# A graph layer with quantile aggregation: neighbour lists and gathered rows in place of sorted tables

## The chip, the core and the metric

The kernel runs on one core of one Trainium2 chip. The core has five engines with instruction streams of their own: PE (TensorE, matrix products into PSUM), DVE (VectorE), ACT (ScalarE), POOL (GpSimd) and SP (SyncE, which here only issues DMAs), and 16 DMA engines. The metric is the device time of one execution in microseconds, as the median of several runs; lower is better.

## What is computed

For 16 graphs (batches) of 1024 nodes with 64 channels: layer norm and relu; then for each node the weighted sum of the 0.25, 0.5 and 0.75 quantiles, per channel, of its kept neighbours' values, itself included; the node's own value is added, a two-layer MLP and a residual follow.

```python
h = jnp.maximum(_layernorm(x, axis=-1), 0.0)
# inside the layer, with x = h:
neigh = (adj_ > 0) & ~eye
rank = jnp.cumsum(ni, axis=-1) - ni
nb = ni.sum(-1)
skip = jnp.where(nb > T, (nb + K - 1) // K, 1)              # T = 10, K = 2
rem = neigh & (sk > 1) & (rank % sk == sk - 1) & mask[:, :, None]
rem = rem | jnp.swapaxes(rem, 1, 2)
adj_d = jnp.where(rem, 0.0, adj_)
vals = jnp.where(nd[..., None], x[:, None, :, :], jnp.inf)
s = jnp.sort(vals, axis=2)
nv = nd.sum(2)
for tau, w in zip((0.25, 0.5, 0.75), (0.25, 0.5, 0.25)):
    pos = tau * (nv - 1)                                      # lo, hi = floor, ceil; frac = pos - lo
    agg = agg + w * (v_lo + frac * (v_hi - v_lo))
y = jax.nn.relu((x + agg) @ W1 + b1) @ W2 + b2
# and at the end
x = x + y * mask
```

The adjacency is a symmetric random one, drawn with probability 1/256 for each direction; a node has 8 neighbours on average.

## The kernel before

It finds the order statistics for any adjacency, with no list of neighbours. For a pair of batches, `prep_pair` does the layer norm (L129 to L143), transposes to channels on 128 partitions, and sorts all 1024 values of each channel with a bitonic network on DVE (L181 to L191, with the node numbers as payload), then sorts back (L216, L217) to give each node's rank. For a batch, `prep_batch` loads the adjacency in 8 tiles of 128 rows (L244), makes it 0 or 0.5 on DVE (L246), clears the diagonal on POOL (L247, `affine_select`), counts neighbours with a scan (L254), marks the dropped edges (L266, L267, L270), puts the diagonal back (L271, POOL) and transposes on PE (L301, L302).

`main` computes a batch in 192 units: 16 groups of four channels, two halves of the nodes and six order statistics. PE multiplies the kept adjacency with weights built from the ranks (`pack`, L374); for each unit `choose`, `words`, `locate` and `add` pick the bucket, select its counts and words (`sel`, L397), move bits (L404), compare (`hit`, L418), weight the hit on POOL (`hitw`, L420), multiply with the candidates (`val`, L422) and sum into `agg` on PE (L426). The units are written as a software pipeline of four stages; one step of the next batch's preparation (`background`) is taken per unit.

The source is written against a layer that places the waits between engines, hands out the buffers (a tile's `bufs` is how many copies of it can be alive) and orders the instructions of each engine when the kernel is built; an engine then works through its own list in that order. DMAs are issued by SP alone. On POOL are the products `wt` (L365) and `hitw`, the coefficients (L339, L340) and the two diagonal masks.

Of the kernel before, what the change touches and what calls it, by code (L numbers as in the profile page):

```python
# [29 lines left out]
I32 = mybir.dt.int32  # L30
U8 = mybir.dt.uint8
AF = mybir.ActivationFunctionType
OP = mybir.AluOpType
AX = mybir.AxisListType

P = 128
N = 1024
C = 64
H = 128
NT = N // P  # L40
NG = 16
NB = 32
HALF = 512
NSEL = 6
WEIGHTS = (0.25, 0.5, 0.25)
EPS = 1e-5
FIELDS = ((0, 11), (11, 11), (22, 10))


@with_exitstack  # L50
def quantile_graph_layer(
# [24 lines left out]
    kb = cst.tile([P, cbf.shape[1]], BF16, name="kb")  # L76
    nc.sync.dma_start(out=kb, in_=cbf)
    kf = cst.tile([P, cf32.shape[1]], F32, name="kf")
    nc.sync.dma_start(out=kf, in_=cf32)
# [30 lines left out]
    # Sorted tables of four groups each, block-diagonal over a group's four channels.  # L110
# [6 lines left out]
    xs, hT, rankT, sorted_d = {}, {}, {}, {}  # L117
    nd, bucket, word_w, maskc = {}, {}, {}, {}

# [1 line left out]
    def prep_pair(pr):  # L121
        xt = wk.tile([P, NT, 2, C], F32, name="xt")
        xs[pr] = xt
        for b in range(2):
            nc.sync.dma_start(out=xt[:, :, b, :], in_=x[2 * pr + b].rearrange("(t p) c -> p t c", p=P))
# [69 lines left out]
        # The sorted values as three bf16 terms.  # L195
# [13 lines left out]
        # Node numbers back in order, each with the place it was found at.  # L209
# [24 lines left out]
    def prep_batch(b):  # L234
        mu = wk.tile([P, NT], U8, name="mu")
        nc.sync.dma_start(out=mu, in_=nodemask[b].rearrange("(t p) -> p t", p=P))
# [5 lines left out]
        for t in range(NT):  # L242
            at = wk.tile([P, N], F32, name="at")
            nc.sync.dma_start(out=at, in_=adj[b, t * P:(t + 1) * P, :])  # L244
# [7 lines left out]
            # Half the inclusive count of neighbours; the dropped ones are those numbered skip, 2 skip.  # L252
# [16 lines left out]
            # 0.5 for a kept edge, 1 for a dropped one, 0 for none.  # L269
# [37 lines left out]
    def main(b, background):  # L307
# [12 lines left out]
        # The order statistics that each node wants, and their weights, on all partitions.  # L320
# [47 lines left out]
        def pack(wt, half):  # L368
            """Counts below (less a half) and the three words, for all buckets of four channels."""
# [25 lines left out]
        def words(packed, hot):  # L395
# [6 lines left out]
            # 2^23 + word: each partition moves its bit to where it reads as 2.0.  # L402
# [69 lines left out]
        nc.sync.dma_start(out=out[b].rearrange("(t p) c -> p t c", p=P), in_=res)  # L472

    def drain(gen):
        for _ in gen:
            pass

    drain(prep_pair(0))
    drain(prep_batch(0))
    for pr in range(B // 2):  # L480
        batch = prep_batch(2 * pr + 1)
        pair = prep_pair(pr + 1) if pr + 1 < B // 2 else iter(())
        main(2 * pr, chain(batch, pair))
        drain(batch)
        # The next pair's first batch takes over what the batch before left free.
        batch = prep_batch(2 * pr + 2) if pr + 1 < B // 2 else iter(())
        main(2 * pr + 1, chain(pair, batch))
        drain(chain(pair, batch))


def constants():
    """Matrices that depend on the shapes alone."""
# [21 lines left out]
    ci32 = np.stack([30 - inside, np.ones(P)], 1).astype(np.int32)  # L514
    return cbf, cf32, ci32
# [25 lines left out]
```

## Time and profile before

| | us |
|---|---|
| median of three runs | 18756.4 |
| lowest and highest run | 18733.7, 18758.3 |
| profiled execution, span from first to last instruction | 18769.8 |

The profile is of one execution. Its first lines give each engine's busy time; its groups give, for a line of the kernel and an engine, the count of instructions, their busy time, the mean duration, and the idle time of the engine ahead of them with what ended it. "128x512 f32" is partitions x elements per partition. A view of a single line gives the shortest, median and longest duration. In a timeline a row is start, duration, engine, line and operation, with the engine's idle time ahead of it in brackets.

### The profile page before, as it was taken

How to read it: one execution, taken by the hardware profiler on the slowest of the kernel's cores; microseconds unless marked ns; L12 is line 12 of the kernel's file. 1: busy time of each engine (PE TensorE's matmuls, PEld its weight loads, DVE VectorE, ACT ScalarE, POOL GpSimd, SP SyncE). 2: the span in 40 equal slices, each digit the busy share in tenths (PEclk: the TensorE clock that was granted, in tenths of full speed). 3: DMA queues.
4: the chain of work that ended last, by engine and by line, in shares of the span. 5: the costliest groups of instructions: out<-in, count | busy, mean ns of one | idle time of the engine just before them, and what ended most of it. 6: DMA issues, size and time to landing. Idle time of an engine off the chain costs nothing. (4 is left out here: it accounts for less than half of the span.)

```text
span 18769.8 us, 153006 instructions
## 1 busy us (share of the span) xinstructions
PE 15007.5 (80%) x55296; PEld 5255.5 (28%) x55296; DVE 15816.9 (84%) x19847; ACT 3137.9 (17%) x5402; POOL 7256.0 (39%) x4293
## 2 busy tenths in 40 slices
PE   2887788777888788887788887888878887788888
PEld 0222222222222222222222222222222222223333
DVE  9898878988789887898878988789887898877777
ACT  0111111111111111111111111111111111111111
POOL 1333443334433344333443334433343333443333
PEclk6999999999999999999999999999999999999999
DMA  0000000000000000000000000000000000000000
GB/s 23 4 1 3 10 8 4 1 3 12 8 2 1 3 12 8 2 1 3 12 8 2 1 3 12 8 2 1 3 12 9 1 2 2 12 6 1 2 1 1
DMA packets 183963, 98.46 MB, mean 5 GB/s; under 512 B 163426, under 2 KB 163618, under 8 KB 183202
## 3 DMA queue, kind: packets, MB, share of 16 engines
q1 hardware_dynamic: 183202, 88.68, 1.8%
q8 instruction: 433, 7.09, 0.2%
q14 instruction: 328, 2.69, 0.0%
HBM read 78.14 MB, written 10.49 MB: 5 GB/s over the span
## 5 line engine op out<-in xcount | busy, mean ns | idle before, releaser
L420 POOL TENSOR_TENSOR hitw<-hit,coef 128x512 bf16<-128x512 bf16 x3072 | 5080.3, 1654 | 9836.9 <-DVE hit L418 9596.5
L426 PE MATMUL agg<-val,kf 128*64 128x512 f32 x6144 | 3445.6, 643 | 2079.5 <-DVE val L422 2071.6
L374 PE MATMUL pk<-kept,wt 128*128 128x512 fp8e4 x16384 | 4170.5, 385 | 278.2 <-POOL wt L365 155.5
L397 DVE TENSOR_TENSOR sel<-packed,hot 128x2048 f16<-128x2048 f16 x3072 | 4090.9, 1335 | 123.3 <-ACT hot L392 115.6
L422 DVE TENSOR_TENSOR val<-cand,hitw 128x512 f32<-128x512 f32 x3072 | 2113.5, 688 | 1976.9 <-POOL hitw L420 1884.2
L401 PE MATMUL wd<-sel,kb 128*128 128x512 f16 x9216 | 2650.1, 391 | 744.4 <-DVE sel L397 742.6
L392 ACT CAST hot<-oh 128x512 f16<-128x512 f32 x3072 | 1797.1, 585 | 7573.1 <-PE oh L390 3841.7
L416 PE MATMUL cand<-hot,table 128*128 128x512 f16 x9216 | 2674.7, 396 | 0.0
L404 DVE TENSOR_SCALAR bits<-wd,ki 128x512 int32<-128x512 int32 x3072 | 2278.7, 742 | 124.4 <-PE wd L401 122.2
L378 ACT ACTIVATE packed<-pk 128x512 f16<-128x512 f32 x2048 | 1223.2, 597 | 6859.8 <-PE pk L374 6858.1
L418 DVE TENSOR_TENSOR hit<-place,want 128x512 bf16<-128x512 f32 x3072 | 2099.5, 683 | 319.2 <-PE place L413 308.0
L374 PEld LDWEIGHTS <-wt 128*128 128x128 fp8e5 x16384 | 1593.4, 99 | 2507.5 <-POOL wt L365 380.5
L365 POOL TENSOR_TENSOR wt<-eq,ww 128x1024 fp8e5<-128x1024 bf16 x768 | 1824.9, 2400 | 724.0 <-DVE eq L362 473.2
L426 PEld LDWEIGHTS agg<-val,kf 128*64 128x64 f32 x6144 | 599.5, 137 | 3576.8 <-DVE val L422 3447.8
L401 PEld LDWEIGHTS <-kb 128*128 128x128 bf16 x9216 | 921.1, 100 | 2088.2 <-issue 1155.6
L413 PE MATMUL place<-bits,kb 128*128 128x512 bf16 x3072 | 1253.2, 408 | 97.9 <-DVE bits L404 96.8
L390 PE MATMUL oh<-below,kb 128*128 128x512 f16 x3072 | 1197.6, 390 | 163.8 <-ACT hot L392 137.9
L383 DVE TENSOR_TENSOR below<-packed,want 128x1536 f16<-128x1536 f16 x1024 | 1254.7, 1225 | 3.9 <-ACT want L337 3.4
L416 PEld LDWEIGHTS <-table 128*128 128x128 bf16 x9216 | 869.5, 100 | 1325.0 <-issue 629.9
L411 PE MATMUL place<-sel,kb 128*128 128x512 f16 x3072 | 1215.8, 396 | 14.6 <-DVE hit L418 14.4
L399 PE MATMUL wd<-hot,kb 128*128 128x512 f16 x3072 | 1200.9, 391 | 0.0
L413 PEld LDWEIGHTS <-kb 128*128 128x128 bf16 x3072 | 304.1, 99 | 1512.5 <-issue 1402.5
(97 smaller groups left out, 7443.2 us busy)
## 6 DMA issues: line engine op xcount, KB each, us to landing
at<-in_adj_dram SPq DMA_DIRECT2D x128, 512.0 KB, 3.6
table<-sd SPq DMA_DIRECT2D x768, 8.0 KB, 1.7
sd<-term SPq DMA_DIRECT2D x24, 256.0 KB, 2.0
xt<-in_x_dram SPq DMA_DIRECT2D x16, 256.0 KB, 4.0
out_dram<-res SPq DMA_DIRECT2D x16, 256.0 KB, 2.6
kb<-in_cbf_dram SPq DMA_DIRECT2D x1, 320.0 KB, 2.7
mu<-in_nodemask_dram SPq DMA_DIRECT2D x16, 1.0 KB, 4.7
kf<-in_cf_dram SPq DMA_DIRECT2D x1, 126.0 KB, 2.6
```

The source lines that it names most:

```text
L365: nc.gpsimd.tensor_tensor(dst(n + 1), eq, wb, OP.mult, saturate=False)
L374: nc.tensor.matmul(pk, wt[:, t, n, :], kept[:, t, half * HALF:(half + 1) * HALF], start=(t == 0), stop=(t == NT - 1),)
L392: nc.scalar.copy(hot, oh)
L397: nc.vector.tensor_tensor(sel, packed, hot[:, None, :].to_broadcast([P, 4, HALF]), OP.mult)
L401: nc.tensor.matmul(wd, fields[n], sel[:, n + 1], start=False, stop=(n == 2))
L404: nc.vector.tensor_scalar(bits, wd.bitcast(I32), shift, 0x40000000, OP.logical_shift_left, OP.bitwise_and)
L413: nc.tensor.matmul(at, prefix, hi, start=False, stop=True)
L416: nc.tensor.matmul(cand, table[g // 4][:, n, g % 4, :], hot, start=(n == 0), stop=(n == 2))
L418: nc.vector.tensor_tensor(hit, at, want[:, half, s], OP.is_equal)
L420: nc.gpsimd.tensor_tensor(hitw, hit, coef[:, half, s], OP.mult)
L422: nc.vector.tensor_tensor(val, cand, hitw, OP.mult)
L426: nc.tensor.matmul(agg[half], pick[:, 60 - 4 * g:124 - 4 * g], val, start=False, stop=(g == NG - 1 and s == NSEL - 1),)
```

## The change

The old code becomes `dense_layer`, which loops over pairs of batches without overlapping them, and stands behind a branch at the end. In front of it comes `list_layer`, which computes all 16 batches from neighbour lists of 24 slots (23 neighbours and the node itself) and sets a flag if a node has 24 or more kept neighbours, or 24 or more occupied blocks of four node numbers. The dense code runs only if the flag is set.

In `list_layer`, for each batch:

- `load`: 8 tiles of adjacency; sign on ACT, diagonal mask on POOL, transposes on PE, back to SBUF in fp8 by ACT; counts by small matmuls.
- `drop`: ranks of the neighbours by matmuls with a triangular matrix, on ACT and DVE turned into the marks of dropped edges.
- `keep`: kept adjacency by matmuls; a matmul packs four node numbers into one key, so that a node's 1024 columns become 256 keys; the 24 largest by three rounds of "maximum of 8" and "replace"; the bits of each key are unpacked to 96 candidates, and a second such selection gives the row numbers `idx` and the coefficients `coef` of the 19 lowest places.
- `normalize`: layer norm; the table of feature rows, with a first row of 3e38 for empty slots, is written to HBM.
- `aggregate`: for each of 8 tiles and 23 slots one indirect DMA of 128 rows, issued by POOL, into `g`; then an exchange network over the slots on DVE, products with `coef`, sums on PE, MLP, residual, store.

`weave` takes 40 steps of the next batch's preparation among the steps of `aggregate`.

```diff
+CAP = 24
+TOP = 19
+SLOTS = CAP + 1
+    def load(b):
+        ne = wk.tile([P, NT, N], FP8, name="ne", bufs=2)
...
+            at = wk.tile([P, N], F32, name="at", bufs=2)
+            nc.sync.dma_start(out=at, in_=adj[b, t * P:(t + 1) * P, :])
+            sg = wk.tile([P, N], BF16, name="sg")
+            nc.scalar.activation(sg, at, AF.Sign)
+            nc.gpsimd.affine_select(
...
+            for s in range(NT):
+                nc.tensor.transpose(tp[:, s], sg[:, s * P:(s + 1) * P], ident16)
+            nc.scalar.activation(ne[:, :, t * P:(t + 1) * P], tp, AF.Relu, saturate=False)
+            yield
...
+    def drop(b):
...
+                nc.scalar.activation(dist[:, n * HALF:(n + 1) * HALF], rk, AF.Abs, bias=bias[:, t:t + 1])
+            nc.vector.tensor_scalar(rem[:, t], dist, half[:, t:t + 1], None, OP.is_equal, saturate=False)
+            yield
+    def keep(b):
...
+            code = psum.tile([P, 2 * P], F32, name="code")
+            nc.tensor.matmul(code, ones16, base, start=True, stop=False)
+            for s in range(NT):
+                nc.tensor.matmul(code[:, 32 * s:32 * s + 32], kept[:, s], nibble, start=False, stop=(s == NT - 1))
+            rest = wk.tile([P, 2 * P], F32, name="rest", bufs=1)
+            left = code
+            for n in range(3):
+                top = keys[:, t, 8 * n:8 * n + 8]
+                nc.vector.max(top, left)
+                if n < 2:
+                    nc.vector.match_replace(rest, top, left, 0.0)
+                    left = rest
+            yield
+        nc.vector.tensor_scalar(over[:, 0, b], keys[:, :, CAP - 1], 256.0, None, OP.is_ge)
...
+        nc.vector.tensor_copy(over[:, 1, b], found[:, :, CAP - 1])
...
+        idx = wk.tile([P, NT, CAP - 1], I32, name="idx")
+        nc.vector.tensor_scalar(idx, found[:, :, :CAP - 1], float(N), 0.0, OP.min, OP.max)
...
+    def aggregate(b):
+        xt, h, htab = feats.pop(b)
+        idx, coef = lists.pop(b), coefs.pop(b)
+        g = wk.tile([P, SLOTS, NT, C], F32, name="g")
+        for t in range(NT):
+            for s in range(CAP - 1):
+                nc.gpsimd.indirect_dma_start(
+                    out=g[:, s, t], out_offset=None, in_=htab,
+                    in_offset=bass.IndirectOffsetOnAxis(ap=idx[:, t, s:s + 1], axis=0),
+                )
+        nc.scalar.copy(g[:, CAP - 1], h)
+        agg = psum.tile([P, NT, C], F32, name="agg")
+        nc.tensor.matmul(agg, ident32, h, start=True, stop=False)
+        yield
+        where, spare = list(range(CAP)), SLOTS - 1
+        for lo, hi, low, high in NETWORK:
+            pa, pb = where[lo], where[hi]
+            if low and high:
+                nc.vector.tensor_tensor(g[:, spare], g[:, pa], g[:, pb], OP.min)
+                nc.vector.tensor_tensor(g[:, pb], g[:, pa], g[:, pb], OP.max)
+                where[lo], spare = spare, pa
+            elif low:
+                nc.vector.tensor_tensor(g[:, pa], g[:, pa], g[:, pb], OP.min)
+            else:
+                nc.vector.tensor_tensor(g[:, pb], g[:, pa], g[:, pb], OP.max)
+            yield
+        for s in range(TOP):
+            v = g[:, where[s]]
+            nc.vector.tensor_tensor(v, v, coef[:, :, s:s + 1].to_broadcast([P, NT, C]), OP.mult)
+            nc.tensor.matmul(agg, ident32, v, start=False, stop=(s == TOP - 1))
+            yield
...
+    def weave(main, steps, side, side_steps):
+        done = 0
+        for n, _ in enumerate(main):
+            while done * steps < (n + 1) * side_steps and side is not None:
+                done += 1
+                if next(side, side) is side:
+                    side = None
...
+    def prepare(b):
+        if b < B:
+            yield from both(drop(b), load(b + 1) if b + 1 < B else iter(()), normalize(b))
+            yield from keep(b)
+    for _ in load(0):
+        pass
+    for _ in prepare(0):
+        pass
+    for b in range(B):
+        weave(aggregate(b), len(NETWORK) + TOP + 5, prepare(b + 1), 40)
...
+def network(n, outs):
+    size = 1 << (n - 1).bit_length()
+    pairs, p = [], 1
+    while p < size:
+        k = p
+        while k >= 1:
+            for j in range(k % p, size - k, 2 * k):
+                for i in range(min(k, size - j - k)):
+                    if (i + j) // (2 * p) == (i + j + k) // (2 * p) and i + j + k < n:
+                        pairs.append((i + j, i + j + k))
+            k //= 2
+        p *= 2
+    live, used = set(outs), []
+    for a, b in reversed(pairs):
+        if a in live or b in live:
+            used.append((a, b, a in live, b in live))
+            live |= {a, b}
+    return used[::-1]
...
+    list_layer(tc, x, adj, nodemask, W1, b1, W2, b2, cbf, cf32, out, flag)
+    full = tc.nc.values_load(flag[0:1, 0:1], min_val=0, max_val=1)
+    with tc.If(full > 0):
+        dense_layer(tc, x, adj, nodemask, W1, b1, W2, b2, cbf, cf32, ci32, out)
```

In `dense_layer` each of 8 loop turns drains `prep_pair`, then for each of two batches drains `prep_batch` and runs `main` with nothing in the background; otherwise its instructions are those of before.

More of the change, by code (lines that the diff above doesn't have):

```diff
@@ L17 @@
 from contextlib import ExitStack
-from itertools import chain
 import concourse.bass as bass
@@ L30 @@
 I32 = mybir.dt.int32
+U16 = mybir.dt.uint16
 U8 = mybir.dt.uint8
@@ L476, in drain @@
             pass
[L478 to L488, printed above, removed]
+    with tc.For_i(0, B, 2) as first:
+        first_b.append(first)
+        drain(prep_pair(0))
+        for b in range(2):
+            drain(prep_batch(b))
+            main(b, iter(()))
@@ new lines, in ones_col @@
+def ones_col(pool, nc):
+    t = pool.tile([P, 1], F32, name="ones_c")
+    nc.vector.memset(t, 1.0)
+    return t
+def network(n, outs):
[16 more added lines that the diff above has]
+    return used[::-1]
@@ new lines, with quantile_graph_layer @@
+NETWORK = network(CAP, range(TOP))
+@with_exitstack
+def quantile_graph_layer(
+    ctx: ExitStack,
+    tc: tile.TileContext,
+    x: bass.AP,
+    adj: bass.AP,
+    nodemask: bass.AP,
+    W1: bass.AP,
+    b1: bass.AP,
+    W2: bass.AP,
+    b2: bass.AP,
+    cbf: bass.AP,
+    cf32: bass.AP,
+    ci32: bass.AP,
+    out: bass.AP,
+):
+    keep = ctx.enter_context(tc.tile_pool(name="keep", bufs=1))
+    flag = keep.tile([1, 1], I32, name="flag")
+    list_layer(tc, x, adj, nodemask, W1, b1, W2, b2, cbf, cf32, out, flag)
+    full = tc.nc.values_load(flag[0:1, 0:1], min_val=0, max_val=1)
+    with tc.If(full > 0):
+        dense_layer(tc, x, adj, nodemask, W1, b1, W2, b2, cbf, cf32, ci32, out)
```

264 lines of the change are left out of this document (252 added, 12 removed).

## The prediction

> **What bounds the kernel now.** I read the head of the page first, then the busy time by stretches, then the waits and the timeline of one stretch inside the main loop.
>
> ```profile
> span 18769.8 us, 153006 instructions
> PE 15007.5 (80%) x55296; PEld 5255.5 (28%) x55296; DVE 15816.9 (84%) x19847; ACT 3137.9 (17%) x5402; POOL 7256.0 (39%) x4293
> ```
> ```profile
> core 0: us, PE busy (x) PEld busy (x) DVE busy (x) ACT busy (x) POOL busy (x), PEclk, DMA share, GB/s
> 0.00:363.80 363.80, 27.85 (x134) 15.36 (x135) 353.03 (x641) 15.70 (x22) 36.39 (x33) 0.56 0.10 27
> 363.80:2660.00 2296.20, 1857.82 (x6806) 644.76 (x6805) 1968.95 (x2446) 387.00 (x669) 906.63 (x530) 0.96 0.02 5
> ```
> ```profile
> DVE val L422 <- POOL hitw L420: 1884.2, 2049, 3.6
> ```
> ```profile
> L397 DVE TENSOR_TENSOR sel<-packed,hot 128x2048 f16<-128x2048 f16 x3072 | 4090.9, 1335 | 123.3 <-ACT hot L392 115.6
> ```
>
> DVE is the bound: 84% of the span, and 1969 of the 2296 us in which the first two batches are computed; PE is close behind. Its largest wait, 1884 us, is for POOL's product `hitw`. The work is 3072 units (16 groups x 2 halves x 6 statistics x 16 batches) of four large DVE instructions each. No DVE time depends on how many neighbours a node has. The span stands 13 us (0.07%) above the median of the runs, 18756.4 us, so the sum below needs no correction.
>
> **What the change removes.** All of it: both sorts, the 3072 units, the packed words. No term of the old kernel stays, so I build the new time from rows. First the rows for DVE and POOL alone and side by side.
>
> ```profile
> 260.12 0.69 DVE L216 TENSOR_TENSOR k<-k 128x512 f32<-128x512 f32 x1
> 260.72 0.69 DVE L217 TENSOR_TENSOR k<-k 128x512 f32<-128x512 f32 x1
> 261.32 0.16 DVE L261 TENSOR_TENSOR second<-skip,many 128x1 f32<-128x1 int32 x1
> 261.39 0.69 DVE L246 TENSOR_SCALAR ne<-at 128x1024 bf16<-128x1024 f32 x1
> ...
> 263.20 0.15 DVE L263 TENSOR_SCALAR first<-second 128x1 f32<-128x1 f32 x1
> 263.47 2.29 DVE L254 TENSOR_TENSOR_SCAN rk<-ne 128x1024 f16<-128x1024 bf16 x1
> ```
> ```profile
> L217 DVE TENSOR_TENSOR k<-k x432: 674/683/2402, 215.6 to 15999.7; 128x512 f32<-128x512 f32 x144
> ```
> ```profile
> L271 POOL TENSOR_SCALAR_AFFINE_SELECT edges<-edges x128: 285/292/3092, 25.5 to 16871.3; 128x128 bf16<-128x128 bf16 x128
> ```
> ```profile
> L247 POOL TENSOR_SCALAR_AFFINE_SELECT ne<-ne x128: 285/946/2214, 13.0 to 16848.2; 128x128 bf16<-128x128 bf16 x128
> ```
> ```profile
> L420 POOL TENSOR_TENSOR hitw<-hit,coef x3072: 1142/1728/3394, 371.7 to 18752.8; 128x512 bf16<-128x512 bf16 x192
> ```
>
> In the timeline two fp32 minimum/maximum instructions on 512 elements start 0.60 us apart, although each is shown with 0.69. A one-column instruction costs 0.07 us of pitch, 0.27 where the next one reads its result (263.20 to 263.47). From (0.60 - 0.07)/512 an fp32 element costs about 1.04 ns.
>
> **DVE per batch.** Working the `network` function through for 24 slots and 19 outputs gives 129 comparators, 124 with both outputs: 253 instructions on 128x512 fp32. 253 x 0.60 = 152 us; 19 products with the coefficients, 11 us; result, 1 us: **164 us**, the main part. Preparation: `keep` has 3 maxima and 2 replacements on 256 elements for each of 8 tiles and the same on 96: 40 x 0.33 + 40 x 0.17 = 20 us, and 0.1 us more for each because it reads what the one before wrote, 28 us. The trace shows no such instruction; as one pass it is this, if a replacement is two passes it is 16 us more. `drop` compares 8 x 1024 elements into fp8: I take the 0.69 of L246, 5.5 us (3 to 10). Layer norm 3, counts 1, keys, indices and coefficients 6: **44 us**. Together 208 us a batch, 190 to 240.
>
> **POOL per batch.** 23 slots x 8 tiles = 184 indirect DMAs, each of 128 rows of 256 bytes, 2944 in all, and 8 diagonal masks. This is the term that decides, and the trace has no DMA issued by POOL. Nearest rows:
>
> ```profile
> L244 SPq DMA_DIRECT2D at<-in_adj_dram x128: 327/328/898, 6.2 to 16768.9; - x128
> ```
> ```profile
> L365 POOL TENSOR_TENSOR wt<-eq,ww 128x1024 fp8e5<-128x1024 bf16 x768 | 1824.9, 2400 | 724.0 <-DVE eq L362 473.2 <-PE pk L374 131.2 <-PE place L413 43.8
> ```
> ```profile
> L315 SPq DMA_DIRECT2D table<-sd x768: 302/430/1575, 206.9 to 17709.3; - x192
> ...
> DMA to landing us min/median/max: 1.5/1.7/3.9
> ```
>
> Below: 0.33 us, SP's issue of a 512 KB load. Above: 2.40 us, POOL's longest group. POOL must read 128 row numbers and make the transfers of 128 rows out of them, which is nearest in kind to `hitw`, POOL going through a few hundred items: 1.14 us undisturbed, 1.73 the median beside DVE. I take the middle, **1.4 us**: 184 x 1.4 = 258 us, plus 8 masks of 1 us (the median of L247) = **266 us a batch** (70 to 450 by the bounds). The landing is no bound: 768 small table loads were issued at 0.43 us each while each took 1.7 us, so several are under way at once. The Trainium skill ("DMA: Bandwidth & Descriptors", section "Anatomy of one DMA — SWDGE (gpsimd) path") gives about 2.0 us plus bytes/436e3 per such DMA; paid one behind the other, that would be an estimated 184 x 2.08 = 382 us a batch. No run here shows it, and the table rows speak against paying it in series.
>
> The other engines have room.
>
> ```profile
> L426 PE MATMUL agg<-val,kf 128*64 128x512 f32 x6144 | 3445.6, 643 | 2079.5 <-DVE val L422 2071.6
> ```
> ```profile
> L301 PE MATMUL et<-kb,edges x1024: 216/219/314, 329.1 to 16930.1; 128*128 128x128 bf16 x171
> ```
> ```profile
> L136 ACT ACTIVATE sq<-h 128x1024 f32<-128x1024 f32 x1 | 1.1, 1061 | 0.0
> ...
> L230 ACT CAST rt<-tp 128x512 f16<-128x512 f32 x2 | 1.2, 586 | 117.8 <-PE tp L229 117.8
> ```
>
> PE: 20 fp32 sums of two passes at 0.64 = 26 us, and some 440 small matmuls at no more than 0.22 = 97 us. ACT: 16 passes over 1024 columns at 1.06 and 36 over 512 at 0.59 = 38 us. SP: 8 loads of 512 KB at 0.33 us. All lie beside POOL; they would show only as latency in the preparation, which I put at 100 us from the adjacency to the row numbers.
>
> **What overlaps.** As written, `weave` puts the last preparation step of batch b+1, which gives the row numbers, some 146 of 153 steps into `aggregate(b)`; kept to that order, gathers and network would follow one another. But the order on an engine is not that of the source: the profile shows that it is planned anew.
>
> ```profile
> 2001.73 0.69 DVE L418 TENSOR_TENSOR hit<-place,want 128x512 bf16<-128x512 f32 x1
> 2002.34 1.22 DVE L397 TENSOR_TENSOR sel<-packed,hot 128x2048 f16<-128x2048 f16 x1
> 2004.59 0.69 DVE L422 TENSOR_TENSOR val<-cand,hitw 128x512 f32<-128x512 f32 x1 [1.04 <-POOL hitw L420]
> ```
>
> The source has `hit`, `val`, then `sel`; on DVE `sel` has moved into the wait for `hitw`. Likewise L246 to L267 of `prep_batch(0)` stand between the passes of the sort that the source finishes first. So I expect that in the wait for the first gathers the next batch's preparation is moved forward; then its gathers follow directly on POOL, into the second `g` buffer, while DVE runs the network. **POOL's issue becomes the bound.** Queued behind the gathers on POOL are the diagonal masks of the load two batches ahead; ACT and PE wait for these, but have more than 100 us of slack.
>
> Sum: 16 x 266 = 4256 us; ahead of the first gather the load and preparation of batch 0, which I estimate at 130 us (8 tiles, each with one load, one rank, one key and one list step of 4, 3, 6 and 3 us, instruction after instruction at the rows above); behind the last gather the network of batch 15 and its MLP, 164 + 12 = 176 us. **4562 us, say 4560**.
>
> The dense code is in the program but runs only if a node has 24 kept neighbours or 24 occupied blocks of four. Counted on the reference's inputs the most are 22 and 22. It then costs one branch.
>
> **The rivals.**
>
> (1) *Short issue, DVE bound.* With 1.1 us or less a gather, DVE's 208 us and a few waits, 218, set the pace: 130 + 202 + 16 x 218 = **3.8 ms**. For it: SP's 0.33 us.
>
> (2) *Half the overlap.* The moved preparation fits only in every second wait: two batches take 208 + 266 + 266 = 740 us, and 8 x 740 + 250 = **6.2 ms**. For it: the row numbers come last in `weave`. Against it: the rows above, where idle time is filled.
>
> (3) *No overlap.* A batch takes 258 + 208 less some 20 us of first comparators: 16 x 446 + 130 = **7.3 ms**.
>
> (4) *POOL held up by DVE.* The masks take 0.29 us alone and 0.95 in the median beside DVE's two-input instructions, and an instruction of DVE that takes 0.68 took up to 2.40. The network is two-input instructions without a gap. If every gather is held up as a mask is, by 0.66 us, it takes 2.06 us and the kernel 16 x (184 x 2.06 + 8) + 306 = **6.5 ms**; held up twice, 2.72 us and 8.4 ms. The Trainium skill ("SBUF — State Buffer", section "Who interferes with whom") has a lock that is held for the whole instruction, against two-input DVE work only while POOL reads SBUF; the long L217 rows agree with a lock. Its section "A bandwidth-pool intuition that's wrong (but worth ruling out)" has a POOL DMA of 0.62 us grow to 3.1 beside a DVE copy: an estimated 16 x 578 + 306 us = 9.6 ms by that figure, and it would speak against overlapping at all.
>
> (5) *The dense code runs too* (slower). One node with 24 kept neighbours decides. A pair then costs the 364 us ahead of the first main part, and two main parts without background, each as long as the last one:
>
> ```profile
> L327 PE MATMUL nv<-kept,kb x256: 376/607/634, 341.0 to 17723.5; 128*128 128x512 fp8e4 x128
> ```
>
> From 17723.5 to the end are 1046 us; 8 x (364 + 2092) = 19.6 ms, with the lists **24 ms**. Against it: the count of 22. For it: a wrong flag would do the same.
>
> **How the numbers follow.** Forecast 0.43; (1) 0.14; (2) 0.15; (3) 0.12; (4) 0.12; (5) 0.04. The forecast's own range, with 1.2 to 1.7 us a gather, is 3.9 to 5.5 ms. The range to hold 8 in 10 takes in (1), (2) and (3): 3600 to 7400 us; left out are (5), the upper half of (4) and issue times over 2.4 us. Faster by over 0.2%, about what a measurement of this kernel can tell from no change: 0.95; within 0.2% nothing lies, 0.01; slower 0.04.
>
> **What would show it.** POOL busy over 80% of the span with gathers 1.4 us apart, no long pause between the gathers of one batch and the next, and DVE waiting for gathers some 60 us a batch: right. DVE idle 250 us in each batch while POOL gathers, POOL idle while the network runs: (3); in every second batch: (2). Gathers that are longer beside the network than in the first batch, where DVE has little to do: (4). DVE over 90% busy: (1). A network instruction of more than 0.7 us would break the DVE sum, a gather under 1.1 or over 1.8 us the POOL sum.

## The result and the profile after

The changed kernel takes **7020 us** (median of 3 runs, 7008.7 to 7024.2) against 18756 us before: a ratio of 0.3743, 95% interval 0.3737 to 0.3750. The forecast was 4560 us with a range of 3600 to 7400. The sign and the range hold, the range only because it was drawn to take in rivals (2) and (3); the forecast's own range ended at 5500 us. The point is 2460 us too low, and the rest of this text asks where those 2460 us went.

From the page of the profile after: the span, the busy times, the chain that ended last, and the costliest groups that matter here.

```profile
span 7022.5 us, 28680 instructions
PE 1409.5 (20%) x8098; PEld 754.4 (11%) x8098; DVE 3262.8 (46%) x6969; ACT 644.6 (9%) x914; POOL 3673.4 (52%) x3076
...
another core or an unknown queue 40%; DVE 29%; issue 11%; POOL 10%; PE 7%; ACT 3%; DMA 0%; SPq 0%; DVEq 0%; ACTq 0%; POOLq 0%
...
L754 POOL DMA_INDIRECT g<-htab,idx x2944 | 2881.5, 979 | 2113.3 <-issue 1338.3
L662 DVE MAX8 keys<-code 128x8 f32<-128x256 f32 x128 | 55.0, 430 | 3318.6 <-remote 2710.9
L766 DVE TENSOR_TENSOR g<-g 128x512 f32<-128x512 f32 x1984 | 1321.0, 681 | 145.7 <-DMA g<-htab,idx 133.9
...
L578 POOL TENSOR_SCALAR_AFFINE_SELECT sg<-sg 128x128 bf16<-128x128 bf16 x128 | 791.7, 6191 | 983.8 <-ACT sg L577 970.9
...
L652 ACT ACTIVATE kept<-kp 128x512 fp8e4<-128x512 f32 x256 | 146.0, 600 | 3501.6 <-remote 2778.8
```

Read it so. DVE works 3262.8 / 16 = 204 us a batch, where 208 were forecast. POOL's gathers last 0.98 us each, with 0.30 us between them: 184 of them take some 235 us, where 258 were forecast. Both main terms are right. But no engine is over 52% busy, so neither of the two engines is the bound: they work **one after the other**. The two largest idle times, in front of DVE's first step on a tile's codes (L662) and of ACT's pass over the kept neighbours (L652), are put down to "remote", a release that the profile cannot assign, and 40% of the chain is "another core or an unknown queue" in a program that runs on one core.

One batch of the changed kernel in four stretches; the columns are the stretch, its length, busy us and instructions of PE, PEld, DVE, ACT and POOL, the granted clock, the DMA share and GB/s.

```profile
3874.00:3920.00 46.00, 20.43 (x124) 11.87 (x123) 25.31 (x49) 12.29 (x20) 35.94 (x34) 0.69 0.48 29
3920.00:4109.00 189.00, 11.37 (x67) 5.83 (x68) 14.63 (x36) 3.47 (x6) 143.26 (x151) 0.50 0.66 26
4109.00:4134.00 25.00, 0.00 (x0) 0.00 (x0) 0.00 (x0) 0.00 (x0) 0.75 (x1) 0.50 0.23 5
4134.00:4334.00 200.00, 57.55 (x315) 32.22 (x315) 169.65 (x364) 24.62 (x31) 87.35 (x8) 0.58 0.08 24
```

From 3874 to 4109 POOL gathers. In the first 46 us the other engines work beside it; then for 189 us DVE does 14.6 us of work and TensorE 67 matmuls. As soon as the gathers are over, DVE works 170 of 200 us, and POOL does eight masks in that time and no gather. The period is 460 us here and 428 on average, 235 of gathers and 193 without: the first gather starts at 105 us, the sixteenth batch's at 6530, (6530 - 105) / 15.

The timeline of POOL in the last stretch shows what eight masks take:

```profile
4144.04 0.29 POOL L578 TENSOR_SCALAR_AFFINE_SELECT sg<-sg 128x128 bf16<-128x128 bf16 x1 [2.87 <-ACT sg L577]
4195.37 84.30 POOL L578 TENSOR_SCALAR_AFFINE_SELECT sg<-sg 128x128 bf16<-128x128 bf16 x2 [51.04 <-ACT sg L577]
4281.54 0.55 POOL L578 TENSOR_SCALAR_AFFINE_SELECT sg<-sg 128x128 bf16<-128x128 bf16 x1 [1.87 <-ACT sg L577]
...
4334.18 2.19 POOL L754 DMA_INDIRECT g<-htab,idx  x1 [45.79 <-DVE at L702]
```

A mask takes 0.29 us alone. In the row of two masks and 84.30 us one is held for 83.5 us, to 4278.91, while DVE runs two-input instructions without a gap. DVE's timeline shows what ends the hold:

```profile
4278.07 0.68 DVE L767 TENSOR_TENSOR g<-g 128x512 f32<-128x512 f32 x1
4278.68 0.25 DVE L686 MAX8 found<-cand 128x8 f32<-128x96 f32 x1
4278.85 0.67 DVE L766 TENSOR_TENSOR g<-g 128x512 f32<-128x512 f32 x1
```

All 15 masks that are held for over 1 us end 0.23 to 0.24 us behind the start of such a maximum of the list building, which reads one input; during the eight longest holds nothing but two-input instructions of the network and the products came before it. So the longer the network runs without a list step in between, the longer the hold.

And the timelines of TensorE, DVE and ACT around the longest idle time in the gathers:

```profile
4009.71 0.37 PE L657 MATMUL code<-kw,kept 128*128 128x32 fp8e5 x7
4011.55 0.18 PE L657 MATMUL code<-kw,kept 128*128 128x32 fp8e5 x1 [1.47 <-issue]
4099.77 0.58 PE L647 MATMUL kp<-ne,kw 128*128 128x512 fp8e4 x1 [88.04 <-issue]
```
```profile
4099.06 0.43 DVE L662 MAX8 keys<-code 128x8 f32<-128x256 f32 x1 [98.72 <-issue]
```
```profile
4099.12 1.08 ACT L652 ACTIVATE kept<-kp 128x512 fp8e4<-128x512 f32 x2 [91.15 <-issue]
```

By the profile TensorE's last matmul on the tile's codes ends at 4011.7; DVE and ACT, which wait for TensorE's signals, start at 4099.1. The signal came **87 us late**. (The ends of matmuls are modelled, so whether the last matmul or only its signal was late the profile can't tell.) Taking for each of the 128 tiles the start of L662 less the end of the tile's last code matmul (or of DVE's instruction before, if that is later), 61 tiles, called *late tiles* below, are over 1 us late, 2953 us in sum, 87.3 at most. Before the late signal the last instructions of a burst leave TensorE 1.40 us apart (weights at 4010.15 and 4012.95, the matmul between them at 4011.55).

So three suspects: the late signals (A), the order of the instructions on DVE (B, later D), and the masks on POOL (C).

### The profile page after: what moved, and what is told of

The parts are those of the page before. It is cut to its first block, busy times and chain, and to the rows that moved or that the text cites. A ratio compares the mean times of both kernels' runs of the same rounds, so it can differ in the third digit from the quotient of the medians.

```text
span 7022.5 us, 28680 instructions
## 1 busy us (share of the span) xinstructions
PE 1409.5 (20%) x8098; PEld 754.4 (11%) x8098; DVE 3262.8 (46%) x6969; ACT 644.6 (9%) x914; POOL 3673.4 (52%) x3076
## 3 DMA queue, kind: packets, MB, share of 16 engines
q0 software_dynamic: 94208, 96.66, 34.0%
## 4 chain that ended last, share of the span: by engine, by line
another core or an unknown queue 40%; DVE 29%; issue 11%; POOL 10%; PE 7%; ACT 3%; DMA 0%; SPq 0%; DVEq 0%; ACTq 0%; POOLq 0%
DVE g L766 11%; DVE g L767 10%; POOL sg L578 7%; POOL g L754 2%; PE agg L777 2%; DVE g L776 2%; DVE keys L662 1%; ACT kept L652 1%; PE yp L795 1%; DVE rest L664 1%; PE rk L630 1%; PE hp L791 1%; DVE found L686 1%; DVE rem L635 1%
## 5 line engine op out<-in xcount | busy, mean ns | idle before, releaser
L754 POOL DMA_INDIRECT g<-htab,idx x2944 | 2881.5, 979 | 2113.3 <-issue 1338.3
L662 DVE MAX8 keys<-code 128x8 f32<-128x256 f32 x128 | 55.0, 430 | 3318.6 <-remote 2710.9
L766 DVE TENSOR_TENSOR g<-g 128x512 f32<-128x512 f32 x1984 | 1321.0, 681 | 145.7 <-DMA g<-htab,idx 133.9
L767 DVE TENSOR_TENSOR g<-g 128x512 f32<-128x512 f32 x1984 | 1322.4, 682 | 7.7 <-DVE g L766 1.4
L578 POOL TENSOR_SCALAR_AFFINE_SELECT sg<-sg 128x128 bf16<-128x128 bf16 x128 | 791.7, 6191 | 983.8 <-ACT sg L577 970.9
L777 PE MATMUL agg<-g,kf 128*128 128x512 f32 x608 | 344.9, 701 | 1185.3 <-DVE g L776 1178.3
L652 ACT ACTIVATE kept<-kp 128x512 fp8e4<-128x512 f32 x256 | 146.0, 600 | 3501.6 <-remote 2778.8
L630 PE MATMUL rk<-kw,ne 128*128 128x512 fp8e5 (+3 forms) x1280 | 359.3, 397 | 14.0 <-issue 13.7
L624 PE MATMUL rk<-kw,ne 128*128 128x128 fp8e5 x1024 | 220.2, 256 | 344.0 <-ACT dist L634 284.1
L776 DVE TENSOR_TENSOR g<-g,coef 128x512 f32<-128x512 f32 x304 | 206.2, 683 | 0.0
L634 ACT ACTIVATE dist<-rk,bias 128x512 f16<-128x512 f32 x256 | 163.0, 688 | 415.4 <-DVE rem L635 285.6
L630 PEld LDWEIGHTS <-ne 128*128 128x128 fp8e4 x1280 | 147.5, 119 | 480.2 <-issue 438.1
L651 PE MATMUL kp<-kw,rem 128*128 128x128 fp8e5 x1024 | 154.2, 289 | 78.8 <-issue 78.8
```

The lines of the kernel that those rows point to most:

```text
L578: nc.gpsimd.affine_select(out=sg[:, t * P:(t + 1) * P], in_=sg[:, t * P:(t + 1) * P], pattern=[[-1, P]], compare_op=OP.not_equal, fill=0.0 ...
L624: nc.tensor.matmul(rk[:, lo * P:(lo + 1) * P], ne[:, s, ts], upper, start=(s == 0), stop=(s == last), skip_group_check=True,)
L630: nc.tensor.matmul(rk[:, lo * P:], ne[:, s, ts], full[:, None, :].to_broadcast([P, 4 - lo, P]), start=(s == 0 and n == 1), stop=False, ski ...
L634: nc.scalar.activation(dist[:, n * HALF:(n + 1) * HALF], rk, AF.Abs, bias=bias[:, t:t + 1])
L652: nc.scalar.activation(kept[:, 4 * n:4 * n + 4], kp, AF.Relu, saturate=False)
L754: nc.gpsimd.indirect_dma_start(out=g[:, s, t], out_offset=None, in_=htab, in_offset=bass.IndirectOffsetOnAxis(ap=idx[:, t, s:s + 1], axis=0),)
```

## The experiments

The results name the chip of each run: e1 to e4 chip 8, e5 to e8 chip 2, e9 and e10 chip 12, e11 and e12 chip 7. It turned out to matter. e10 and e12 were run four times, the others once. The kernel before took 18757 to 18771 us on all four. No chip is named for the runs of the changed kernel above. The table has what all runs gave; the last columns are the late tiles, and the signals of DVE's main semaphore that the trace holds of those that its instructions name.

| run | us | chip | gathers | late tiles (sum us) | signals held of named |
|---|---|---|---|---|---|
| changed kernel | 7020 | not named | 184 a batch | 61 (2953) | 5911 of 6391 |
| e1 no gather | 3367 | 8 | none | 0 | all |
| e2 rows from SP | 3476 | 8 | none, plain DMAs | 0 | all |
| e3 half the gathers | 5216 | 8 | 92 | 28 (984) | 6030 of 6381 |
| e4 lists first | 6036 | 8 | 184 | 0 (no gather beside the lists) | 5677 of 6304 |
| e5 16 rows each | 5567 | 2 | 184 | 0 | 6385 of 6393 |
| e6 masks on DVE | 5749 | 2 | 184 | 0 | all |
| e7 plain DMAs on POOL | 3492 | 2 | none | 0 | all |
| e8 pairs of slots | 5695 | 2 | 184 | 0 | all |
| e9 one network at a time | 4899 | 12 | 184 | 0 | 6390 of 6394 |
| e10 e9 and e6 | 4504 | 12 | 184 | 0 | 6507 of 6509 |
| e11 pause on POOL | 6906 | 7 | 184 | 96 (2355) | 5581 of 6394 |
| e12 e10 and pairs | 6238 | 7 | 184 | 27 (1005) | 4168 of 4698 |

**e1, no gather.**

```diff
-                nc.gpsimd.indirect_dma_start(
...
-        nc.scalar.copy(g[:, CAP - 1], h)
+        for s in range(CAP):
+            nc.scalar.copy(g[:, s], h)
```

> All 24 slots of g are filled from h by ACT copies, so no gather is issued and the output is not the reference's; everything else stays. Theory A (TensorE crawls at 1.40 us per instruction while gathers run, which starves the ACT and DVE work of the list building and makes gathers and network run one after the other): the 235 us window goes, the batch falls to DVE's own 204 us plus some waits, 3.5 to 4.1 ms in all, and no stretch has TensorE instructions 1.4 us apart. Theory B (the planned order on DVE, with list building between the network's steps, stalls DVE whatever the gathers do): over 5 ms. Theory C (POOL's masks held up by DVE's two-input work set the time): the masks stay held up, 790 us of POOL's time remain, and the time stays over 4.5 ms.

3367 us, and DVE is the bound: busy 3230.7 us, 96% of the span. The order on DVE, the 8 masks on POOL and TensorE's 506 matmuls a batch cost next to nothing when no gather runs. Theories B and C fall as causes *by themselves*; whatever the order does, it needs the gathers' duration to do it. That DVE is busy does not by itself hold the masks: DVE is busier here than in the changed kernel, and no mask takes more than 9.1 us.

```profile
L578 POOL TENSOR_SCALAR_AFFINE_SELECT sg<-sg x128: 292/526/9140, 24.0 to 2628.2; 128x128 bf16<-128x128 bf16 x128
```

**e2, the same rows from SP's queue.**

```diff
-                nc.gpsimd.indirect_dma_start(
...
+                nc.sync.dma_start(out=g[:, s, t], in_=htab[1 + t * P:1 + (t + 1) * P])
```

> Each of the 184 gathers of a batch becomes a plain DMA of the same 128 rows of 256 bytes, issued from SP's queue with fixed addresses; POOL then makes no descriptors (the output is not the reference's). Theory A1 (the crawl comes from POOL's making of descriptors): no crawl, 3.5 to 4.3 ms, or the time that SP's issue takes if that is longer. Theory A2 (the crawl comes from the traffic of small packets on the DMA engines): TensorE instructions are again about 1.4 us apart in the loading windows and the time stays within 10% of the changed kernel's 7020 us if a window is as long as now.

3476 us, DVE 93% busy, no late tile, although 2944 DMAs brought the same 96.66 MB, on the chip on which e3 has 28 late tiles. Neither the bytes nor the number of DMAs makes signals late; it takes the indirect form or POOL's queue, and which of the two this run can't tell.

**e3, half the gathers.**

```diff
-        for t in range(NT):
+        for t in range(NT // 2):
...
+            nc.scalar.copy(g[:, s, NT // 2:], h[:, NT // 2:])
```

> Only the first 4 of the 8 node tiles are gathered (92 gathers per batch), the rest of g is filled from h by ACT (the output is not the reference's). Theory A: the window halves from 235 to about 118 us, and as windows and network follow one another, the period of 440 us falls by about 118 us: 5.0 to 5.4 ms. The forecast's own view (POOL's issue is hidden or is the bound): with POOL at 130 us a batch, DVE bounds and the time is under 4.2 ms. Theory B (order on DVE): over 6 ms.

5216 us, as A has it. 92 gathers a batch less took 1805 us, 113 us a batch, close to their own 92 x 1.25 = 115 us, as if the gathers stood in the chain with their full length. The match is in part chance, since the late tiles fell from 2953 to 984 us and the masks grew from 792 to 1032. The forecast's view, under 4.2 ms, falls.

**e4, all lists first.** The lists and counts of 16 batches are kept, and normalisation and coefficients are moved into the second stage.

```diff
-        weave(aggregate(b), len(NETWORK) + TOP + 5, prepare(b + 1), 40)
+    for b in range(B):
+        for _ in prepare(b):
+            pass
...
+        weave(aggregate(b), len(NETWORK) + TOP + 5, side, 4)
```

> The lists of all 16 batches are built first, with no gather running; then come the gathers and networks, batch after batch, with the normalisation and the coefficients of the next batch beside them. The output is the reference's. Theory A: TensorE runs fast in the first stage (65 to 115 us a batch, 1.0 to 1.8 ms), and in the second stage the gathers follow one another on POOL, 235 to 250 us a batch, with the 164 us of DVE's network beside them: 3.8 to 4.0 ms; with head and tail 5.1 to 6.0 ms, so faster than 7020 us. Theory B or C (the list building is slow by itself, or masks held by DVE): the first stage takes over 3 ms and the sum is 7 ms or more. If the network itself is slowed by the gathers, the second stage has a period over 350 us.

6036 us, just above what A said. The first stage takes 690 us, 43 a batch, faster than expected. But the second stage has a period of 322 us, not 240, and there only gathers and networks are left. Something other than late signals for the lists parts gathers and networks; A is not the whole cause.

**e5, 16 rows in each gather.**

```diff
-                    out=g[:, s, t], out_offset=None, in_=htab,
-                    in_offset=bass.IndirectOffsetOnAxis(ap=idx[:, t, s:s + 1], axis=0),
+                    out=g[:THIN, s, t], out_offset=None, in_=htab,
+                    in_offset=bass.IndirectOffsetOnAxis(ap=idx[:THIN, t, s:s + 1], axis=0),
```

> Every one of the 184 gathers of a batch is kept, but fetches 16 rows in place of 128 (the rest of g is filled from h by ACT; the output is not the reference's). It parts the number of gathers from the number of descriptors. If the crawl goes with the descriptors that POOL makes (an eighth of them left): no lasting crawl, POOL's pitch well below 1.25 us, 3.4 to 4.0 ms. If it goes with the gather instructions as such: TensorE again about 1.4 us per instruction while they run; with a pitch of 1 us or more the window stays near 200 us and the time over 5.5 ms.

```profile
L757 POOL DMA_INDIRECT g<-htab,idx x2944 | 2879.1, 978 | 1978.8 <-issue 1639.7
```

The shortest, median and longest gather, here and in the changed kernel:

```profile
L757 POOL DMA_INDIRECT g<-htab,idx x2944: 842/847/29022, 104.1 to 5329.3; - x197
```
```profile
L754 POOL DMA_INDIRECT g<-htab,idx x2944: 942/947/2212, 105.1 to 6769.8; - x197
```

5567 us. The means, 978 ns for 16 rows and 979 for 128, are alike by chance: here more of the gathers ran beside DVE's work. Where DVE idles they are 0.85 and 0.95 us, as the medians show. An eighth of the rows saves a tenth of the time: POOL's price is nearly all by DMA. That the time stays over 5.5 ms was taken as the sign of the second theory, but it isn't one: no tile is late, and on this chip none is late with 128 rows either (e6, e8). It leaves the rows' part in the late signals open, and shows a period of 333 us without any of them.

**e6, masks on DVE.**

```diff
-            nc.gpsimd.affine_select(
-                out=sg[:, t * P:(t + 1) * P], in_=sg[:, t * P:(t + 1) * P], pattern=[[-1, P]],
...
+            nc.vector.tensor_tensor(sg[:, t * P:(t + 1) * P], sg[:, t * P:(t + 1) * P], off, OP.mult)
```

> The diagonal masks of the adjacency tiles go from POOL (affine_select, up to 169 us for one while DVE ran its network) to DVE, as one product with a constant per tile, 128 of some 0.15 us; the gathers stay. The output is the reference's. Theory A: the crawl and the windows stay, and only the share of the chain that the masks held (7%, about 520 us) can go: 6.3 to 7.0 ms. Theory C (the held-up masks are what spreads the batch to 440 us): under 5.5 ms.

5749 us, below what A and above what C expected. One period of it, with the columns as above, is what led on:

```profile
2456.00:2546.00 90.00, 41.88 (x342) 24.83 (x341) 85.33 (x200) 33.18 (x48) 71.58 (x54) 0.73 0.56 70
2546.00:2686.00 140.00, 0.00 (x0) 0.00 (x0) 0.00 (x0) 0.00 (x0) 105.85 (x112) 0.50 0.69 25
2686.00:2709.00 23.00, 0.00 (x0) 0.00 (x0) 21.10 (x34) 0.00 (x0) 17.43 (x18) 0.50 0.59 28
2709.00:2811.00 102.00, 39.34 (x164) 18.12 (x165) 98.46 (x213) 5.49 (x9) 0.00 (x0) 0.62 0.07 7
```

The list building runs beside the gathers at full speed (342 matmuls in 90 us). Then nothing is left to do but a network: DVE idles for 140 us until the gathers land, works 102 us alone, and POOL stands still until it is done, although `g` has two buffers. The order in which the instructions stand on DVE says why. Counted in it, batch by batch, for the changed kernel and for e6 (network and products, 272 a batch; b+1 starts with its first instruction that waits for gathers):

```
                    left of b when b+1 starts / of b+1 ahead of the end of b
changed kernel      102 / 55, 91 / 46, 100 / 53, 93 / 48  (four batches)
e6                  90 / 46, 88 / 44, 90 / 46, 88 / 44
```

Some 45 instructions of the **next** network stand ahead of the last 90 of this one. DVE takes its instructions in order; the next network's wait for the next gathers, so the last 90 wait too; and only they free the buffer that the gathers after the next want.

**e7, plain DMAs on POOL.**

```diff
-                nc.gpsimd.indirect_dma_start(
...
+                nc.gpsimd.dma_start(out=g[:, s, t], in_=htab[1 + t * P:1 + (t + 1) * P])
```

> Each gather becomes a plain DMA of 128 rows of 256 bytes with fixed addresses, still issued on POOL's queue (the output is not the reference's). With the run that issued them on SP (3476 us) it parts the indirect form from POOL's queue. If anything that POOL issues in software makes the crawl: TensorE at 1.4 us per instruction in the windows and 5.5 to 7.5 ms. If only the indirect form does: under 4.2 ms.

3492 us; 545 ns for one, where the indirect form takes 979. On this chip no run has late signals, so on these it says nothing. POOL is busy 54% of the span and DVE, at 93%, is the bound.

**e8, pairs of slots**, on top of e4; `pick` takes two slots at once, 1024 elements, and `free` two spare ones.

```diff
-                nc.vector.tensor_tensor(g[:, spare], g[:, pa], g[:, pb], OP.min)
+                nc.vector.tensor_tensor(pick(free), va, vb, OP.min)
```

> On top of the version with all lists first, two exchanges of one layer are done by one DVE instruction of 1024 elements where the places of their slots allow it: 140 network instructions per batch in place of 253, the same elements (the output is the reference's). In the run with lists first DVE got through 162 instructions, 101 us of work, in a window of 240 us, and the period was about 325 us. If the crawl is a price per instruction (about 1.4 us each in a window), 140 + 19 + some 12 instructions fit nearly whole into a window: period 245 to 275 us, 4.7 to 5.3 ms. If the gathers slow DVE's work by its elements (101 us of work per window), the 170 us of work still need 70 us beyond the window: 5.8 to 6.1 ms.

5695 us, a period of 302 us after the lists: neither theory's number. The reason that both gave for e4's 322 was wrong; the order on DVE is planned here as in the changed kernel (in the last batches 55 to 68 of the 159 instructions of network and products are left when the next one starts), and that would set the period, though no run mends the order of this kernel.

**e9, one network at a time.** An order of issue on DVE is added, and no wait:

```diff
+            if ends:
+                tc.add_manual_dep(
+                    ins, ends[0],
...
+        ends[:] = [last.name]
```

> The changed kernel with one thing added: each network instruction of a batch is ordered on DVE behind the last product of the batch before (an order of issue, no wait on another engine). As planned before, some 50 network instructions of batch b+1 stood on DVE ahead of the last 70 to 100 of batch b; they wait for the gathers of b+1, and the rest of b, which frees the buffer for the gathers of b+2, waits behind them. Theory D (this order makes gathers and network follow one another): the gap on POOL that comes from it, some 90 to 100 us per batch, goes: 5.3 to 6.0 ms with the masks still held up on POOL, and less if TensorE's late signals go with it. Theory A (TensorE's late signals alone set the period): within 3% of 7020 us.

4899 us, below all that was expected, with the masks still on POOL, and these now take 0.30 us each (38.2 us for 128). No instruction of the next network stands ahead of the end of this one, and the pause on POOL between the last gather of one batch and the first of the next, 179 to 224 us in the later batches of the changed kernel and some 102 in e6, is 33 us. Its first 18 go to the eight masks, which wait for ACT's signs; the rest is a wait for TensorE's sums:

```profile
2716.04 0.29 POOL L578 TENSOR_SCALAR_AFFINE_SELECT sg<-sg 128x128 bf16<-128x128 bf16 x1 [1.50 <-ACT sg L577]
2732.25 0.94 POOL L756 DMA_INDIRECT g<-htab,idx  x1 [15.92 <-PE agg L790]
```

**e10, this order and the masks on DVE**: the edits of e9 and e6 together.

> The same order of networks, with the diagonal masks on DVE as in the run before that moved them (5749 us). The output is the reference's. Theory D: nothing but the gathers stands on POOL and the buffer is free when they want it, so the period falls from 350 us to POOL's own 184 gathers of 1.25 to 1.37 us, 230 to 252 us: with head and tail of some 400 us 4.2 to 4.6 ms, the sum of the forecast. If the gap of 100 us between two windows has another cause (the lists come late, DVE's 208 us cannot lie beside the gathers): 5.4 to 5.9 ms.

**4504 us** (4498 to 4509), a ratio of 0.2401 to the kernel before, 95% interval 0.2397 to 0.2405: theory D's number, and the fastest version of the study. From its page, and one period of it:

```profile
span 4503.9 us, 28620 instructions
...
POOL 69%; issue 19%; DMA 5%; DVE 4%; PE 1%; ACT 1%; SPq 0%; POOLq 0%; DVEq 0%; ACTq 0%
...
L755 POOL DMA_INDIRECT g<-htab,idx x2944 | 3281.1, 1114 | 1012.7 <-issue 887.4
L766 DVE TENSOR_TENSOR g<-g 128x512 f32<-128x512 f32 x4048 | 2767.4, 687 | 948.5 <-DMA g<-htab,idx 884.1
```
```profile
2450.00:2500.00 50.00, 35.03 (x287) 21.52 (x286) 44.33 (x97) 21.40 (x35) 38.13 (x35) 0.85 0.62 49
2500.00:2600.00 100.00, 11.63 (x84) 7.09 (x82) 96.97 (x236) 12.77 (x14) 81.53 (x61) 0.53 0.55 52
2600.00:2716.00 116.00, 34.36 (x134) 14.70 (x135) 70.15 (x112) 4.65 (x8) 88.87 (x90) 0.59 0.60 29
```

The chain is now POOL's gathers and the 0.30 us between them, 88%. DVE works its 211 us beside them and waits 884 / 16 = 55 us a batch for gathers. A gather lasts 1.17 us on average beside DVE's work and 0.94 where DVE idles, 1.11 over all; with the time between them 184 of them make the period of 265 us, 1.44 us each. Between two batches POOL no longer pauses: the first gather of one follows the last of the other after 0.3 us.

**e11, a pause on POOL** in the changed kernel: a memset of 128x64 behind each gather.

```diff
+                pause[:] = [nc.gpsimd.memset(spin, 0.0).ins]
+                behind(pause[0], fetch)
```

> The changed kernel, its order on DVE as planned, with a small memset (128x64) put behind each gather on POOL, so that the gathers go out more slowly; the output is the reference's. In the changed kernel DVE's first step on a tile's codes started over 1 us after TensorE's last matmul of that tile in 61 of 128 tiles, 2974 us in all; in the runs where DVE worked beside the gathers and these were 1.3 to 1.45 us apart there was none. If the late signals need gathers at full rate (1.25 us): none or few are late at a pitch of 1.4 us or more, and although POOL has more to do the time falls to 5.6 to 6.3 ms (theory D's gap stays). If they go with gathers beside masks on POOL whatever the rate: 40 or more late, and 7.2 ms or more.

6906 us, and 96 tiles late (2355 us) at a pitch of 1.41 us, where the changed kernel has 2953 us (the 2974 of the expectation) at 1.28 on average. Signals are late at the slower rate too. The time is neither theory's.

**e12, e10 with pairs of slots**: the edits of e10 and the one of e8.

> The version of 4503 us with two exchanges of one layer in one DVE instruction where the slots allow it (140 network instructions per batch in place of 253, the same elements; the output is the reference's). POOL is its bound: 184 gathers 1.44 us apart, against 1.25 where DVE idled. If the gathers are stretched by the number of DVE's instructions, their pitch falls to 1.30 to 1.36 us: 4.1 to 4.3 ms. If by the time that DVE is at work on two-input operations (nearly the same): 4.4 to 4.52 ms.

6238 us (6206 to 6351), a ratio of 0.3318 (0.3306 to 0.3330), outside both expectations: late signals are back. Whether pairs of slots gain anything stays open. But this run tells something else. Up to its first network e12 has on TensorE, on DVE and on POOL the same instructions in the same order as e10, and so has e9 as the changed kernel. The first gathers start at 105 to 107 us in all four, and no network runs yet. Two stretches of 20 us each, in the order changed kernel, e9, e12, e10:

```profile
120.00:140.00 20.00, 3.03 (x21) 1.64 (x21) 2.17 (x7) 1.20 (x2) 15.12 (x17) 0.50 0.78 21
140.00:160.00 20.00, 1.53 (x6) 0.46 (x4) 0.00 (x0) 0.60 (x1) 15.12 (x17) 0.50 0.53 29
```
```profile
120.00:140.00 20.00, 10.98 (x119) 6.38 (x116) 19.04 (x81) 3.92 (x8) 15.12 (x17) 0.85 0.71 22
140.00:160.00 20.00, 0.00 (x0) 0.00 (x0) 7.16 (x44) 1.51 (x2) 15.13 (x17) 0.50 0.55 29
```
```profile
120.00:140.00 20.00, 3.34 (x25) 2.07 (x22) 0.23 (x1) 1.04 (x2) 15.08 (x16) 0.50 0.85 48
140.00:160.00 20.00, 1.57 (x10) 0.67 (x10) 0.00 (x0) 0.60 (x1) 15.10 (x16) 0.50 0.56 30
```
```profile
120.00:140.00 20.00, 19.94 (x223) 13.20 (x222) 19.35 (x70) 16.30 (x25) 15.43 (x16) 1.00 0.81 75
140.00:160.00 20.00, 13.64 (x108) 8.93 (x107) 14.56 (x79) 13.92 (x19) 14.31 (x15) 0.83 0.70 151
```

The same instructions beside the same gathers: 25 matmuls in 20 us or 223, and the first network starts at 681 us in e12 and at 324 in e10. In e6, which also has e10's instructions up to there but ran on chip 2, it starts at 321. (In e9 TensorE is through with the lists at 140 us, its next loads waiting for masks behind the gathers.) The table sorts itself by chip: where 128-row gathers run beside the list building, the runs on chips 8 and 7 have late signals and lose records of signals, those on chips 2 and 12 have none and lose next to none.

## Why the prediction was right in its sign and wrong in its point

**DVE's sum** held: 204 us a batch against 208, a network instruction at 0.68 us (0.60 apart), and the new instructions close to their estimates (a maximum of 256 elements 0.43 us, a replacement 0.085 + 0.41).

**POOL's gathers** held: 1.25 us apart where DVE idles, 1.43 beside its work, 1.4 forecast. The bounds from SP's issue (0.33) and POOL's longest group (2.40) were far off on both sides. That the point came so near is in part luck: it was the middle of 1.14 and 1.73, two times of another instruction. The Trainium skill's sum in series ("DMA: Bandwidth & Descriptors", section "Anatomy of one DMA — SWDGE (gpsimd) path"), an estimated 382 us a batch, the trace contradicts: 235 to 265.

**The masks** were mis-sized: 8 us a batch forecast, 791.7 / 16 = 49 measured, single ones held up to 169 us. Rival (4) named the place and aimed at the wrong instruction: beside the network the gathers grow by a quarter (0.94 to 1.17 us), the masks are held until DVE comes to an instruction that lets them in. With the order mended the masks' place on POOL still costs 4899 - 4504 = 395 us on one chip, and there it is the queue and not the hold: no mask lasts over 0.84 us, but the next gathers stand behind masks that wait for ACT.

**"Its gathers follow directly on POOL, into the second `g` buffer, while DVE runs the network"** is the step that failed. The reading that the order is planned anew, and that idle time is filled, was right, and this is what undid it: the wait for the gathers was filled not only with the next lists but also with the head of the next network, placed ahead of the tail of this one, in a queue that goes in order. The two buffers were then worth one for the last 90 instructions. The prediction looked at what moves forward into a wait and not at what is left behind it. e9 and e10 change this order and nothing else in the network, and e10 against e6 is 5749 - 4504 = 1245 us. These two ran on two chips, both without late signals, and start their first network within 3 us of each other, so the chip does not explain it; what goes is POOL's pause of some 102 us a batch, while a batch's gathers grow from some 251 to 265 us, because DVE now works beside them. With order and masks mended the time is 4504 us; that this is so near the forecast's 4560 is in part luck, since the forecast counted the masks on POOL.

**"ACT and PE have more than 100 us of slack"** failed where signals are late: 2953 us over 16 batches are 185 us a batch, up to 87 for one tile. e12 against e10, 1734 us, is the best measure of it, if pairs of slots cost nothing. The three parts overlap (a held mask and a late list fill the same pause) and do not add up to 2460 in any one way; the changed kernel was not run on a chip known to be without late signals. By e5 and e6 it would take some 5.5 to 5.8 ms there, an estimate.

**Rival (3)**, no overlap, has the time (7.3 ms) and its marker, DVE idle while POOL gathers and POOL idle while DVE works; its reason, that the source order is kept, is not the cause.

**What stays open** is what makes the signals late. In the burst shown some 30 instructions of TensorE, 15 matmuls and 15 weight loads, start within 5 us, the last three 1.40 us apart, and then the engine stands for 87 us; no run shows the reason. Records of signals are missing in the same runs, and every run here has its core's span and clock on record, so whether the lateness comes with the recording is not known. That the chip decides is argued from the grouping: no kernel was run on two of them, and the runs of one chip were also taken at one time, so that the time of the runs would fit as well.

## What to carry to other kernels

Two buffers overlap only as far as the consumer's instructions stand in the order in which the buffers fill: where a planner fills a wait, look at what it leaves behind that wait on an in-order engine, and order the end of one use ahead of the start of the next. A price per engine is not a schedule: after the sums, follow who frees the buffer. Before comparing two variants, look whether the same instructions at the same place, ahead of the edit, took the same time; if they did not, something other than the edit differs.

## What the runs showed of the hardware that was not expected

- An indirect DMA on POOL costs nearly the same for few rows: 0.85 us for 16 rows and 0.95 for 128 where DVE idles; a plain one of 128 rows on the same queue takes 0.545.
- A POOL instruction that reads and writes SBUF can be held for the whole of a run of two-input DVE instructions, 84 to 169 us for a mask of 0.29, and gets in at the next maximum, 0.23 us behind its start. The Trainium skill ("SBUF — State Buffer", section "Who interferes with whom") has a lock that is held for the whole of one instruction; the trace has POOL held over more than a hundred DVE instructions back to back. The indirect DMAs on the same queue were stretched only from 0.94 to 1.17 us on average.
- Signals between engines came up to 87 us late while indirect DMAs ran, in the runs on some chips and not in those on others, with the kernel before at the same time on all of them (18757 to 18771 us).
